# Scan units of 16 states by 63 positions in place of 8 states by 127

## The chip, the cores and the metric

The kernel runs on one core of one Trainium2 chip. The core has five engines with queues of their own: TensorE (PE in the profile, its weight loads PEld), VectorE (DVE), ScalarE (ACT), GpSimdE (POOL) and SyncE (SP, which here only issues DMAs). The metric is device time in microseconds, lower is better. Before the change the median of 3 runs is 32431.41 us (32428.44 to 32433.08).

## The reference

Input x is (8, 56, 56, 192), float32. The first layer (a gated Toeplitz convolution along rows and along columns, between two normalisations) is not touched by the change. The second is a selective scan in eight directions over the 3136 positions of each image. Cut to what matters, with DI = 384 channels, N = 16 states, K = 8 directions:

```python
def _selective_scan(u, delta, A, Bs, Cs, D):
    h0 = jnp.zeros(u.shape[:3] + (A.shape[-1],), u.dtype)
    def step(h, inp):
        ul, dl, bl, cl = inp
        dA = jnp.exp(dl[..., None] * A)
        h = dA * h + (dl * ul)[..., None] * bl[:, :, None, :]
        y = jnp.einsum('bkdn,bkn->bkd', h, cl)
        return (h, y)
    _, ys = jax.lax.scan(step, h0, (uL, dL, BL, CL))
```

u are the 384 channels after a 3x3 convolution, in the order of one direction; delta (softplus of a projection), B and C (16 values per position each) come from projections of u. Every channel has 16 states, each a first order recurrence along the positions. y, the states weighted with C and summed over the 16, goes on to a sum over directions, a layer norm, a gate and a projection.

## The kernel before, in words

**Stages.** The first layer takes the first tenth of the span. Then for each of the 8 images there is a scan stage (lines 484 to 922) and a layer norm stage (926 on), which writes the result and prepares the next image. The change is in the scan stage alone.

**Tiling of the scan.** Channels lie on partitions in NB = 3 blocks of 128. Positions are cut into chunks of W = 127, 25 in a direction; 4 chunks make a `Group` (7 groups in a direction, the last of one chunk). A `Unit` (710) is one chunk of one channel block with half of the states: 8 states by (1 + 127) positions, 1024 columns, the extra column holding the state before the chunk. A `Pair` (673) is two chunks of one channel block, so 4 units. One direction has 150 units, an image 1200, the kernel 9600. Units run pair after pair: both halves of chunk 0, both halves of chunk 1, then the next channel block.

**One unit, engine by engine.** PE makes the products delta\*u\*B (`products`, 716): the moved operand `bd` holds B on diagonals, the stationary operand `dut` holds delta\*u turned with positions on partitions, so a matmul over 64 positions spreads them to (states, positions). Positions 0 to 63 use partitions 0 to 63 (row group 0), the rest partitions 64 to 126 (row group 1). The result `bx` is 1024 float32 columns, two banks of PSUM; bank 0 holds states 0 to 3, bank 1 states 4 to 7, so each row group has something to write into both banks. The unit is therefore made in two turns of two matmuls: in turn 0 row group 0 writes bank 0 and row group 1 bank 1, in turn 1 the other way about. An ACT instruction stands between the turns (`turns_part`, 743, and `between`): it waits for turn 0, and turn 1 waits for it. ACT makes the decays `da` = exp(delta\*A) (line 687, one instruction a state and pair) and copies the state before the chunk into column 0 of every state of `bx` (`before`, 755); at the end of a pair it also keeps the last state in `carry` (`keep`, 773). DVE runs the scan (760) from `da` and `bx` into `h`. POOL multiplies `h` by C, spread over all partitions in `cbt`, into `hc` (`times_c`, 778). PE sums over states by 8 accumulating transposes (`sums`, 788) into `yps`, which ACT copies out (698) and SP stores to DRAM (708), 127 rows of 384 values each.

**What sets the order.** The order is written out by hand: a loop over steps t (871) emits, for every engine, parts of different units: turn 1 of unit t+1, turn 0 of unit t+2, the sums of unit t-3, `before` of unit t+1, the scan of unit t, `times_c` of unit t-1. Each engine runs its own instructions in that order and waits on semaphores. Exponentials are placed by a credit: 2.4 a step, 0.4 for each, less for other ACT work. `bx` has 3 buffers, `h` and `hc` 4, `da` 4, `dut` and `bd` 5, `cbt` 3, `yps` two halves of one bank, and one PSUM bank (`pmisc`) serves all other products.

**The front of a group** is planned by `Group.plan` (642) at steps before the group's first unit: load of `xs` (532), three projections `px` (539, copied out at 552), `to_dram` and `broadcast` of C (557, 563), B written to DRAM on diagonals (`diagonal_out`, 630, elements of 4 bytes) and read back (`diagonal_in`, 636), three matmuls `pd` for delta (574, copied out at 583), softplus (587), delta\*u on POOL (611), its transposes on PE (616) and the copy into `dut` (620). `do("SP", t)` puts the DMAs of a step behind its stores in SP's one queue.

Of the kernel before, what the change touches and what calls it, by code (L numbers as in the profile page):

```python
# [62 lines left out]
N = 16  # L63
# [3 lines left out]
NI = 10  # L67
W = 127
NG = -(-L // (4 * W))

# [14 lines left out]
def conv_kernel(ctx: ExitStack, tc: tile.TileContext, a: dict, out: bass.AP):  # L85
# [311 lines left out]
    for b in range(B):  # L397
# [86 lines left out]
        with ExitStack() as st:  # L484
            one = st.enter_context(tc.tile_pool(name="scan1", bufs=1))
            pre = st.enter_context(tc.tile_pool(name="front", bufs=2))
            blk = st.enter_context(tc.tile_pool(name="blk", bufs=5))
            hp = st.enter_context(tc.tile_pool(name="hp", bufs=4))
            cbp = st.enter_context(tc.tile_pool(name="cbp", bufs=3))
# [5 lines left out]
            das = [one.tile([128, 2, HN, W + 1], F32, name=f"da{i}") for i in range(4)]  # L495
            for t in das:
                nc.gpsimd.memset(t[:, :, :, 0], 0.0)
            yps = pyp.tile([W, 2, 2, 128], F32, name="yps")
# [3 lines left out]
            class Group:  # L502


                def __init__(self, k, g, i):
                    self.k, self.g, self.i = k, g, i
                    self.place, self.o, self.rev = DIRS[k]
                    self.nch = 4 if g < L // (4 * W) else 1
                    self.n = self.nch * W
                    u0 = g * 4 * W  # L510
                    self.m = min(self.n, L - u0)
                    self.p0 = L - u0 - self.m if self.rev else u0
                    self.ns = (self.nch + 1) // 2
                    self.ncs = self.nch // self.ns
                    self.w2 = self.ncs * W
                    self.cb, self.dut, self.bd = [], [], []
                    self.tag = "" if self.nch > 1 else "_last"
# [36 lines left out]
                def to_dram(self):  # L554
                    self.cd = cdp.tile([2, N, 2 * W], F32, name="cd")
                    for s in range(self.ns):
                        nc.sync.dma_start(
                            self.cd[s, :, : self.w2], self.pxs[48 : 48 + N, s * self.w2 : (s + 1) * self.w2]
                        )

                def broadcast(self, s):
                    cbt = cbp.tile([128, N, 2 * W], F32, name="cbt")
                    nc.sync.dma_start(
                        cbt[:, :, : self.w2],
                        self.cd[s : s + 1, :, : self.w2].to_broadcast([128, N, self.w2]),
                    )
# [3 lines left out]

# [19 lines left out]

# [16 lines left out]
                def product(self, c):  # L607
                    part = slice(c * W, (c + 1) * W)
                    xs = self.xs[:, :, ::-1] if self.rev else self.xs
                    self.du = pre.tile([128, NB, W], F32, name="du")  # L610
                    nc.gpsimd.tensor_mul(self.du, self.delta[:, :, part], xs[:, :, part])  # L611

                def turn(self, c):
                    self.pt = pmisc.tile([W, 512], F32, name="pt", tag="misc")
                    for d in range(NB):
                        nc.tensor.transpose(self.pt[:, d * 128 : (d + 1) * 128], self.du[:, d], ident)  # L616

                def turned(self, c):
                    dut = blk.tile([W, DI], F32, name="dut")
                    nc.scalar.copy(dut, self.pt[:, :DI])  # L620
                    self.dut.append(dut)

                def diagonal_out(self, c):
                    image = bdd[(self.i + c) % NI]
                    for h in range(2):
                        nr = min(64, W - 64 * h)
                        to = image[h]
                        to = bass.AP(to.tensor, to.offset, [[64, N], [64 * N + 1, nr], [1, 1]])
                        u = c * W + 64 * h
                        nc.sync.dma_start(  # L630
                            to, self.pxs[32 : 32 + N, u : u + nr].rearrange("n (s o) -> n s o", o=1)
                        )

                def diagonal_in(self, c):
                    bd = blk.tile([128, N, 64], F32, name="bd")
                    nc.sync.dma_start(
                        bd.rearrange("p n j -> p (n j)"),
                        bdd[(self.i + c) % NI].rearrange("h (s x) -> (h s) x", s=64),
                    )
                    self.bd.append(bd)  # L640

                def plan(self, at):

                    f = self.first

                    if self.nch == 1:
                        for d in range(NB):
                            at("PE", f - 23, self.project, d)
                        at("ACT", f - 22, self.projected)
                        at("SP", f - 22, self.to_dram)  # L650
                        at("PE", f - 21, self.all_steps)
                        at("late", f - 20, self.all_stepped)
                        start, out = f - 18, f - 22
                    else:
                        for d in range(NB):
                            at("PE", f - 22 + d, self.project, d)
                            at("PE", f - 18 + 2 * d, self.steps, d)
                            at("ACT", f - 17 + 2 * d, self.stepped, d)
                        at("ACT", f - 19, self.projected)
                        at("SP", f - 19, self.to_dram)  # L660
# [662 lines left out]
```

## Time and profile before

| what | value |
|---|---|
| median of 3 runs | 32431.41 us |
| span of the profiled execution | 32431.7 us |
| mean granted TensorE clock, core 0 | 0.974 |
| scan stage of one image, first to last scan (8 of them) | about 3125 us |
| busy share of the span: PE, DVE, ACT, POOL | 92%, 74%, 72%, 69% |
| DMA busy share in the scan stage, data rate | 0.43, 125 GB/s |
| DMA packets, all / under 512 bytes | 4696313 / 3677488 |

```profile
## 2 busy tenths in 40 slices
PE   8999899989999899989999899989998899989998
DVE  3444588858887588848887688848886688858886
ACT  2333588848887588848887588848886688848886
POOL 0000488838887588838887588838886688838885
```

The page cuts the span into 40 slices of some 811 us; a digit is the busy share of an engine in tenths. The first four slices are the first layer. After that the pattern repeats for eight images: 3 to 4 slices of scan, in which all engines but SP are at 0.8 or more, and a dip where the layer norm stage lies. Groups of instructions in the page have: line, engine, operation, output and inputs with partitions and elements, count, busy time and mean duration in ns of one, and the idle time of the engine just before them with what ended most of it. A timeline row has start and length in us, engine, line, what is done and how many instructions are merged in it; in brackets the idle time before it.

### The profile page before, as it was taken

To read this page: it belongs to the slowest core of one execution; us is meant where nothing else is said; L and a number is where in the kernel's file an instruction comes from. 1 tells how busy PE (TensorE), PEld (TensorE's weight loads), DVE (VectorE), ACT (ScalarE), POOL (GpSimd) and SP (SyncE) were. 2 spreads that over 40 slices of the span, in tenths; PEclk is the share of its full clock that TensorE was granted. 3 is DMA by queue.
4 is the path that set the end of the run, shared out by engine and by line. 5 is a ranking of instruction groups with operands and counts; after the bars stand their busy time and mean duration, and the time that the engine had idled before them with its cause. 6 is when DMAs were issued, how large, how long until landed. Compare 5 with 4: busy or idle time off the path is not lost. (4 is left out here: it accounts for less than half of the span.)

```text
span 32431.7 us, 535874 instructions
## 1 busy us (share of the span) xinstructions
PE 29974.2 (92%) x195376; PEld 20574.4 (63%) x195376; DVE 23854.0 (74%) x13460; ACT 23290.3 (72%) x63667; POOL 22357.6 (69%) x11632
## 2 busy tenths in 40 slices
PE   8999899989999899989999899989998899989998
PEld 5555566656666566656666566656666566656666
DVE  3444588858887588848887688848886688858886
ACT  2333588848887588848887588848886688848886
POOL 0000488838887588838887588838886688838885
PEclk9999999989999999989999999989999999999999
DMA  3222344444444444444444444444444444444444
GB/s 79 60 60 57 104 124 127 128 134 127 128 123 129 131 128 125 129 132 125 127 128 128 130 128 125 127 133 128 125 129 126 131 127 128 126 133 129 124 127 140
DMA packets 4696313, 3931.67 MB, mean 121 GB/s; under 512 B 3677488, under 2 KB 4379376, under 8 KB 4587824
## 3 DMA queue, kind: packets, MB, share of 16 engines
q1 hardware_dynamic: 4660528, 3890.16, 41.8%
q8 instruction: 1552, 25.43, 0.3%
q10 hardware_dynamic: 33152, 7.23, 0.2%
q14 instruction: 1081, 8.86, 0.1%
HBM read 3402.49 MB, written 508.64 MB: 121 GB/s over the span
## 5 line engine op out<-in xcount | busy, mean ns | idle before, releaser
L760 DVE TENSOR_TENSOR_SCAN h<-da,bx 128x1024 f32<-128x1024 f32 x9600 | 21446.0, 2275 | 3899.2 <-ACT bx L755 2988.2
L778 POOL TENSOR_TENSOR hc<-h,cbt 128x1016 f32<-128x1016 f32 x9600 | 20685.7, 2175 | 2449.0 <-DVE h L760 1924.3
L687 ACT ACTIVATE da<-delta,A_logs 128x254 f32<-128x254 f32 x39936 | 17114.9, 490 | 832.0 <-PE bx L732 785.1
L732 PE MATMUL bx<-bd,dut 63*128 63x252 f32 (+1 forms) x76800 | 11022.8, 404 | 1053.0 <-ACT bx L755 377.1
L788 PEld LDWEIGHTS yps<-ident,hc 128*127 128x127 f32 x76800 | 9249.2, 190 | 3383.4 <-issue 2106.3
L788 PE MATMUL yps<-ident,hc 128*127 128x128 f32 x76800 | 11068.5, 287 | 196.9 <-ACT bx L755 143.1
L732 PEld LDWEIGHTS bx<-bd,dut 64*128 64x128 f32 (+1 forms) x76800 | 6510.0, 187 | 4511.0 <-ACT da L687 876.4
L422 POOL MEMSET xp<- 128x58 f32 x12 | 1.3, 192 | 3406.1 <-DMA bd<-none 3406.1
L611 POOL TENSOR_TENSOR du<-delta,xs 128x381 f32<-128x381 f32 x1600 | 1602.1, 1002 | 745.2 <-ACT bx L755 478.8
L1022 POOL COPY xo<-xp 128x672 f32<-128x672 f32 x98 | 70.5, 749 | 2841.8 <-ACT xp L1005 2841.8
L539 PE MATMUL px<-xs,xpw 128*64 128x508 f32 (+1 forms) x2688 | 1304.9, 576 | 171.5 <-DMA xs<-xo 171.5
L574 PE MATMUL pd<-pxs,dtw 13*128 13x508 f32 x2304 | 1295.2, 641 | 18.2 <-ACT delta L583 10.7
L583 ACT COPY delta<-pd 128x508 f32<-128x508 f32 x1152 | 669.3, 581 | 726.4 <-PE pd L574 720.5
L755 ACT COPY bx<-h 128x8 f32<-128x8 f32 x4608 | 753.9, 164 | 592.7 <-PE bx L732 320.6
L773 ACT COPY carry<-h 128x8 f32<-128x8 f32 x4608 | 884.2, 192 | 343.4 <-DVE h L760 328.0
L755 ACT COPY bx<-carry 128x8 f32<-128x8 f32 x4992 | 820.7, 164 | 412.9 <-PE bx L732 381.9
L1005 ACT ACTIVATE xp<-pc,conv_b 128x448 f32<-128x448 f32 x147 | 93.5, 636 | 1352.1 <-PE pc L998 1352.0
L998 PE MATMUL pc<-xp,dg 128*128 128x448 f32 x2646 | 1019.5, 538 | 0.0
L698 ACT COPY yt<-yps 127x256 f32<-127x256 f32 (+1 forms) x2496 | 888.3, 356 | 154.3 <-PE yps L788 98.6
L1142 DVE SCALAR_TENSOR_TENSOR y<-xc,dsum,ysum 128x224 f32<-128x224 f32 x336 | 125.4, 443 | 1132.3 <-PE ysum L1123 1132.3
L620 ACT COPY dut<-pt 127x384 f32<-127x384 f32 x1600 | 757.9, 474 | 167.5 <-PE pt L616 123.6
L616 PE MATMUL pt<-ident,du 128*127 128x128 f32 x4800 | 815.7, 279 | 52.1 <-POOL du L611 36.2
(136 smaller groups left out, 16257.3 us busy)
## 6 DMA issues: line engine op xcount, KB each, us to landing
cbt<-cd SPq DMA_DIRECT2D x768, 2032.0 KB
bd<-bd SPq DMA_DIRECT2D x1600, 512.0 KB
yk<-yt SPq DMA_DIRECT2D x3584, 84.0 KB
xs<-xo SPq DMA_DIRECT2D x384, 762.0 KB
yt<-yt SPq DMA_DIRECT2D x1536, 190.5 KB
xo<-xo SPq DMA_DIRECT2D x168, 672.0 KB
cbt<-cd SPq DMA_DIRECT2D x64, 1016.0 KB
lt<-td SPq DMA_DIRECT2D x32, 1568.0 KB
```

The lines of the kernel that those rows point to most:

```text
L539: nc.tensor.matmul(self.px[:, : self.n], weights[self.k][0][:, d], self.xs[:, d], start=(d == 0), stop=(d == NB - 1),)
L574: nc.tensor.matmul(self.pd[:, : self.n], weights[self.k][1][:, d * 128 : (d + 1) * 128], self.pxs[0 : R + 1], start=True, stop=True,)
L611: nc.gpsimd.tensor_mul(self.du, self.delta[:, :, part], xs[:, :, part])
L687: yield nc.scalar.activation(da[:, : G.ncs, n, 1:], src.rearrange("p (c t) -> p c t", t=W), AF.Exp, scale=an[:, G.k, self.d, col : col + 1],)
L698: nc.scalar.copy(G.yt[:, : G.ncs, self.d * 128 : (self.d + 1) * 128], yps[:, self.i % 2, : G.ncs])
L732: mm = nc.tensor.matmul(self.bx[:, 4 * q : 4 * q + 4, 1 + 64 * r : 1 + 64 * r + nr], dut[rows, P.d * 128 : (P.d + 1) * 128], bd[rows, n0 : ...
L755: return nc.scalar.copy(self.bx[:, :, 0], prev)
L760: nc.vector.tensor_tensor_scan(self.h.rearrange("p n t -> p (n t)"), das[2 * (P.i % 2) + self.half][:, self.c].rearrange("p n t -> p (n t) ...
L773: nc.scalar.copy(P.carry[:, P.d, states(self.half)], self.h[:, :, W])
L778: nc.gpsimd.tensor_tensor(self.hc, self.h[:, :, 1:], G.cb[P.s][:, states(self.half), self.c * W : (self.c + 1) * W], ALU.mult,)
L788: nc.tensor.matmul(yps[:, self.P.i % 2, self.c], lhsT=self.hc[:, n], rhs=ident, start=(self.half == 0 and self.c == 0 and n == 0), stop=(s ...
L998: nc.tensor.matmul(pc, dg[:, d, j, :], xp[:, d, t * RT + dy : t * RT + dy + RT, dx : dx + HW], start=(j == 0), stop=(j == 8),)
```

## The change

W becomes 63, a chunk 63 positions (50 in a direction), a group 8 chunks. A unit now holds all 16 states of one chunk and channel block: again 16 x (1 + 63) = 1024 columns, and again 150 units in a direction. Two chunks form a pair for the front: `dut` has the first chunk in partitions 0 to 62 and the second in 64 to 126, and a copy with these halves exchanged (`swapped`) is made by two DMAs. `bd` is filled so that partitions 0 to 63 hold states 0 to 7 and partitions 64 to 127 states 8 to 15, for both chunks. So row group 0 makes states 0 to 7 of a unit, all in bank 0, and row group 1 states 8 to 15, all in bank 1: two matmuls of 504 columns, no turns, no ACT instruction between them.

The three channel blocks are interleaved, each one chunk behind the one before, so that a unit's predecessor in its own chain is three units back. `before` copies 16 columns from its `h` directly; `carry` and `keep` are gone. A block of exponentials covers 4 chunks of one channel block (252 elements an instruction, as before 254), and `da` is four times 4 chunks by 16 states. `hc` of two successive units lies side by side, so that one transpose of 126 columns sums both; 16 of them for two units, 8 a step. `yps` is copied out once for 4 units, and each unit's 63 rows of 128 values are stored by a DMA of their own.

Counts in one full group of 24 units, before and after: product matmuls 96 of 256 or 252 columns and 48 of 504; transposes for the sums 192 and 192; copies `before` 24 and 24 (8 and 16 columns); `keep` 12 and 0; exponentials 96 and 96; copies of `yps` 6 and 6; DMAs on SP: `diagonal_out` 8 and 8, `diagonal_in` 4 and 8, `swapped` 0 and 8, `broadcast` 2 and 4 (half the size), stores 4 and 24, `to_dram` 2 and 1, load 1 and 1.

```diff
-W = 127
-NG = -(-L // (4 * W))
+W = 63
+NC = -(-L // W)
+GC = 8
+NG = -(-NC // GC)
+SC = 4
...
-            blk = st.enter_context(tc.tile_pool(name="blk", bufs=5))
+            blk = st.enter_context(tc.tile_pool(name="blk", bufs=3))
             hp = st.enter_context(tc.tile_pool(name="hp", bufs=4))
+            hcp = st.enter_context(tc.tile_pool(name="hcp", bufs=3))
...
-            das = [one.tile([128, 2, HN, W + 1], F32, name=f"da{i}") for i in range(4)]
+            das = [one.tile([128, SC, N, W + 1], F32, name=f"da{i}") for i in range(4)]
...
-            yps = pyp.tile([W, 2, 2, 128], F32, name="yps")
+            yps = pyp.tile([2 * W, 2, 2, 128], F32, name="yps")
...
+                def swapped(self, p):
+                    dut = self.dut[p][0]
+                    other = blk.tile([128, DI], F32, name="dus")
                     for h in range(2):
+                        nc.sync.dma_start(other[64 * h : 64 * h + 64], dut[64 - 64 * h : 128 - 64 * h])
+                    self.dut[p].append(other)
...
+                        x = f - 24
+                        for d, s in enumerate((f - 18, f - 16, f - 12)):
+                            at("PE", s, self.steps, d)
+                            at("ACT", s + 1, self.stepped, d)
+                        at("late", f - 10, self.softplus)
+                    at("SP", x - 12, self.load)
+                    for d in range(NB):
+                        at("PE", x + d, self.project, d)
+                    at("ACT", x + 3, self.projected)
+                    at("SP", x + 3, self.to_dram)
+                    for p in range(self.npr):
+                        at("SP", x + 3 + p, self.diagonal_out, p)
+                        s = f - 8 + 6 * p
+                        at("POOL", s - 1, self.product, p)
+                        at("PE", s, self.turn, p)
+                        at("ACT", s + 1, self.turned, p)
+                        at("SP", s + 1, self.swapped, p)
+                        at("SP", s + 1, self.diagonal_in, p)
+                        at("SP", f + 6 * p - 5, self.broadcast, p)
...
+                def products(self):
+                    G, p, q = self.G, self.c // 2, self.c % 2
+                    self.bx = pb.tile([128, 2, HN, W + 1], F32, name="bx")
                     for r in range(2):
-                        q = (r + turn) % 2
-                        n0 = self.half * HN + 4 * q
-                        nr = min(64, W - 64 * r)
-                        rows = slice(64 * r, 64 * r + nr)
-                        mm = nc.tensor.matmul(
-                            self.bx[:, 4 * q : 4 * q + 4, 1 + 64 * r : 1 + 64 * r + nr],
-                            dut[rows, P.d * 128 : (P.d + 1) * 128],
-                            bd[rows, n0 : n0 + 4, :nr],
+                        rows = slice(64 * r, 64 * r + W)
+                        nc.tensor.matmul(
+                            self.bx[:, r, :, 1:],
+                            G.dut[p][q ^ r][rows, self.d * 128 : (self.d + 1) * 128],
+                            G.bd[p][rows, q, :, :W],
                             start=True,
                             stop=True,
                         )
-                        if turn:
-                            tc.add_manual_dep(mm.ins, self.between, IN_TURN, reason="bank")
...
+            for t in range(-2, len(units) + 10):
                 credit = min(credit, 0.0) + 2.4
                 if (U := unit(t + 2)) is not None:
-                    U.products(0)
+                    U.products()
+                for U, y in stores:
+                    U.store(y)
+                stores = []
+                for i in range(t, t + 3):
+                    U = unit(i)
+                    if U is not None and not U.ready and (U.prev is None or U.prev.h is not None):
+                        U.before(U.prev)
+                        credit -= 0.2
+                s = t - 4
+                if unit(s) is not None:
+                    if s % 2 == 0:
+                        sums(s, 0)
+                    else:
+                        sums(s - 1, 1)
+                        hcs.pop(s // 2)
+                s = t - 8
+                if unit(s) is not None and s % 4 == 0:
+                    y = pre.tile([2 * W, 2, 128], F32, name="yt")
+                    nc.scalar.copy(y, yps[:, s // 4 % 2])
                     credit -= 0.35
+                    stores = [(units[s + i], y[i % 2 * W : i % 2 * W + W, i // 2]) for i in range(4)]
                 credit -= 0.5 * do("ACT", t)
...
                 while must_exp(t):
                     one_exp()
+                while credit > 0.8 and may_exp(t):
+                    one_exp()
                 do("DVE", t)
                 if (U := unit(t)) is not None:
                     U.scan()
                 do("PE", t)
                 if (U := unit(t - 1)) is not None:
+                    if (t - 1) % 2 == 0:
+                        hcs[(t - 1) // 2] = hcp.tile([128, N, 2, W], F32, name="hc")
+                    U.times_c(hcs[(t - 1) // 2][:, :, (t - 1) % 2])
                 do("POOL", t)
                 do("SP", t)
```

## The prediction

> **What bounds the kernel now.** I read the stretches of the scan stage first, then the groups of instructions, then the timeline of single engines.
>
> ```profile
> 7286.00:10411.00 3125.00, 2977.11 (x20428) 2111.42 (x20427) 2680.48 (x1200) 2707.47 (x7629) 2766.19 (x1411) 1.00 0.43 125
> ```
>
> The columns are stretch, length, busy us of PE, PEld, DVE, ACT, POOL, clock, DMA share, GB/s. One image's scan takes 3125 us, 2.604 a unit. PE is busy 95% of it, the others 86 to 89%: PE is nearest to its limit, and four engines lie close together. Eight images: 25000 us.
>
> ```profile
> L760 DVE TENSOR_TENSOR_SCAN h<-da,bx 128x1024 f32<-128x1024 f32 x9600 | 21446.0, 2275 | 3899.2 <-ACT bx L755 2988.2 <-ACT da L687 383.9 <-PE bx L732 272.4
> L773 ACT COPY carry<-h 128x8 f32<-128x8 f32 x4608 | 884.2, 192 | 343.4 <-DVE h L760 328.0
> L755 ACT COPY bx<-h 128x8 f32<-128x8 f32 x4608 | 753.9, 164 | 592.7 <-PE bx L732 320.6 <-DVE h L760 255.0
> ```
>
> The scan stands idle 3899 us, three quarters of it for the 0.16 us copy into column 0, and that copy waits for products and an earlier scan. So a cheap link of a chain through three engines ends last.
>
> ```profile
> 10015.49 1.13 PE L732 MATMUL bx<-bd,dut 64*128 64x256 f32 x8
> 10016.55 1.15 PE L788 MATMUL yps<-ident,hc 128*127 128x128 f32 x8
> 10017.63 1.13 PE L732 MATMUL bx<-bd,dut 64*128 64x256 f32 x8
> 10018.69 1.15 PE L788 MATMUL yps<-ident,hc 128*127 128x128 f32 x8
> 10019.68 0.50 PE L616 MATMUL pt<-ident,du 128*127 128x128 f32 x3
> 10020.10 1.13 PE L732 MATMUL bx<-bd,dut 64*128 64x256 f32 x8
> ...
> 10030.18 0.70 PE L732 MATMUL bx<-bd,dut 64*128 64x256 f32 x4
> 10032.06 0.70 PE L732 MATMUL bx<-bd,dut 64*128 64x256 f32 x4 [1.19 <-DVE h L760]
> 10033.20 1.12 PE L788 MATMUL yps<-ident,hc 128*127 128x128 f32 x8 [0.44 <-ACT bx L755]
> ...
> 10040.18 1.07 PE L539 MATMUL px<-xs,xpw 128*64 128x508 f32 x2
> 10041.17 1.13 PE L732 MATMUL bx<-bd,dut 64*128 64x256 f32 x8
> ...
> 10049.78 1.11 PE L574 MATMUL pd<-pxs,dtw 13*128 13x508 f32 x2
> 10050.82 1.13 PE L732 MATMUL bx<-bd,dut 64*128 64x256 f32 x8
> ```
>
> By starts: products 1.06 us, sums 1.08, a plain unit 2.14; a turn adds 0.33 (2.47 from 10017.63 to 10020.10), px 0.99, pd 1.04. At 10030 the two turns (x4 each, where elsewhere x8 run through) fall apart, and PE waits.
>
> **PE's own sum.** A direction is 150 x 2.14 = 321.0 us; six full groups of 3 x 0.99 + 3 x 1.04 + 4 x 0.33 = 7.41 make 44.5; the short group has 0.80 + 0.86 + 0.33 = 2.0 (starts in its own rows near 9954 and 9959). 367.5 us, times 64: 23520. PE waits 25000 - 23520 = 1480 us. That is the most this change can take from waits; below it PE's work itself stands.
>
> ```profile
> 10032.99 6.64 DVE L760 TENSOR_TENSOR_SCAN h<-da,bx 128x1024 f32<-128x1024 f32 x3 [0.99 <-ACT da L687]
> 9942.74 21.32 POOL L778 TENSOR_TENSOR hc<-h,cbt 128x1016 f32<-128x1016 f32 x10
> 10042.36 3.29 ACT L687 ACTIVATE da<-delta,A_logs 128x254 f32<-128x254 f32 x8 [0.21 <-PE bx L732]
> ```
>
> Undisturbed, scans follow at (6.64 - 2.29) / 2 = 2.18 us, elsewhere up to 2.25: some 21100 us. POOL: (21.32 - 2.17) / 9 = 2.13, with 1600 products of 1.00 some 22050. Exponentials: (3.29 - 0.49) / 7 = 0.40; with copies, table loads and softplus ACT has some 327 us a direction, 20900. All below PE.
>
> **The change, part by part.**
>
> *Products.* Row groups overlap: single records at 10006.27, .59, .81 and 1.02 later carry one pass of each row group, 0.213 us for 256 columns, so 1.06 is 0.11 for the first weights, four passes and 0.10 to drain. Now two passes of 504 columns, 0.42 each: 1.05. Gain 0.015 x 9600 = 140 us.
>
> The kernel issues both passes of row group 0 before those of row group 1, and the records of the two first passes start 6 ns apart. The Trainium skill (TensorE: Matmul & The Clock Gate, Part 3) says that matmuls start and end strictly in program order. By that rule row group 1 starts only with the other's second pass, and a unit takes three passes, 1.46 us; the row disagrees, and my sum does without the rule.
>
> *The turns and the ACT instruction between.* This wait goes. Three `bx` buffers let PE begin unit t+3 when scan t ends; DVE then has two units, 4.4 us, and products with copy need some 1.4. So 3.0 us of lateness are covered, where before turn 0, an ACT instruction, turn 1 and the copy had to fit into one scan. Since PE's sum is above DVE's, DVE eats its stock and waits for PE; PE waits for nobody. I take back all 1480, less what follows.
>
> *Chains.* The predecessor ends three units earlier, so the copy of column 0 waits for its products alone. It is queued ahead of the exponentials on ACT: they stand behind it while PE makes the products. 16 columns for 8: between nothing and another 0.16 us; an exponential of 254 elements takes 0.49, so I take 0.01, hidden in ACT's slack. `keep` gone: 4608 x 0.10 us, off the path: 0 (460 gained if ACT were the bound). ACT after: 320 us a direction of PE's 365.
>
> *`yps`.* Its halves share a bank. The copy is queued behind the sums of the next pair, the second half of these sums behind the copy. ACT stands some 0.9 us per copy, 37 a direction, 33 us: 353 of 365, still covered, but hardly.
>
> *Softplus.* With its table loads 1.28 + 1.47 + 1.28 = 4.03 us on ACT, against 0.35 spare a step: ACT is 3.7 late. Where a `yps` copy stands behind it, the sums can absorb about 1.9, and PE waits 1.8; this falls so in half of the directions. 384 x 0.9 = 350 us; bounds 0 and 384 x 4.03 = 1550.
>
> *Short groups.* 48 exponentials of 0.32, softplus 3.05 and copies 1.8 are 20.3 us of ACT in six units, where PE has 14.8: 5.5 x 64 = 350; bounds 0 and twice that.
>
> *POOL.* Runs of 63 in place of 127, 16 for 8. No row shows the price of a run. A copy of 672 elements in 12 runs takes 749 ns, so a run costs between 0 and 62 ns; I take 6, 0.05 a unit: 2.35 with the products, under PE's 2.43.
>
> *DMAs.*
>
> ```profile
> L708 SPq DMA_DIRECT2D yt<-yt x1600: 216/531/6541, 3706.9 to 32157.5; - x178
> L630 SPq DMA_DIRECT2D bd<-pxs x3200: 303/677/7692, 3637.6 to 32092.0; - x189
> 10020.37 17.80 SPq L708 DMA_DIRECT2D yt<-yt x3
> ```
>
> SP issues 54 a group in place of 21. By medians (0.53 a store, 0.68 `diagonal_out`, 0.55 the reads and, as nearest row, the swaps, 0.76 `broadcast`, 3.6 the load) that is 34 us of 58. `swapped` waits for ACT's copy, with reads and broadcast queued behind it; landing is due five steps, 12 us, later. Cost 0; without cover see the second rival.
>
> *Ends of an image.* Sixteen exponentials before the first scan in place of eight, 3.2 us, a swap, and chains that run out: some 8 us x 8 = 60.
>
> **Sum.** 32431.7 - 25000 + 23520 - 140 + 350 + 350 + 60 = 31570 us. The span, 32431.7, is the median of 32431.41 but for 0.3. The sum's own range, with softplus and short groups between their bounds for the most part, is 31100 to 32150.
>
> **Rivals.**
>
> *ACT takes PE's place.* For: 353 of 365 us, and copies that block the exponentials behind them. Against: ACT late no longer idles. If each step loses 0.25 us more, a direction is 391, as now (25000 / 64): 32450.
>
> *SP late, the slower side.* The three stores at 10020 held SP 5.9 us each; the mean of a queue that backs up decides. From 58 / 54 = 1.08 us SP is the bound, from 62.5 / 54 = 1.16 the kernel is slower; at 1.3, twice the medians, a full group is 70 us, 6.25 x 64 of them 28000, the time 35400. Against: 127 rows of a store trickled over 16 us at a DMA share of 0.07, one engine's worth; 63 rows can be split evenly.
>
> *Row groups in series.* 1.46 in place of 1.05: 9600 x 0.41 = 3900, 35500. Against: the row groups overlap now, and nothing but the length differs.
>
> *POOL's runs.* From 17 ns a run POOL is the bound, from 38 the kernel is slower, at 62 it has 2.80 a unit: 26900, time 34300.
>
> *No waits at all.* 30870, if ACT's lags are absorbed.
>
> **How the numbers follow.** Forecast 0.60; no waits 0.08; ACT 0.10; SP 0.08; POOL 0.05; series 0.04; a wait I haven't seen, slower, 0.05. Two in a thousand, 65 us, is what this measurement can tell from no change. Faster: 0.58 + 0.08 + 0.04 (ACT) + 0.02 (POOL) = 0.72; same 0.05; slower 0.23. The range 30850 to 32700 leaves out most of the slower rivals, some 0.17, and little below.
>
> **What would show it.** Right: products of some 1.05 us in four records, PE above 97% busy in the scan stage, the scan's idle time released by products or copies at PE's pace, stages of about 3000 us. Wrong: scans or sums that wait for DMAs or POOL, SP issues with a mean over 1.1 us, `times_c` above 2.3 us, products above 1.2, or PE rows with gaps released by the copy of `yps`.

## The result and the profile after

The changed kernel takes 34835.51 us (median of 4 runs, 34818.07 to 34856.32), the kernel before beside it 32431.65 us: a ratio of 1.0742, with a 95% interval of 1.0727 to 1.0758. The forecast was 31570 us. The change costs 2404 us where it was to save 860.

First the stretches, as before. The columns are stretch, length, busy us of PE, PEld, DVE, ACT and POOL with their instructions, granted clock, DMA share, GB/s. The first row is the scan stage of the second image; the others are groups 0 to 3 of one direction (24 units each), from the start of one scan to that of another.

```profile
7595.02:11022.04 3427.02, 3007.93 (x15604) 1598.81 (x15604) 2653.87 (x1199) 2611.32 (x7031) 2737.52 (x1403) 0.94 0.48 125
...
12802.44:12899.38 96.94, 67.80 (x312) 34.96 (x310) 53.03 (x26) 55.12 (x149) 57.44 (x30) 0.85 0.35 95
12899.38:12978.82 79.44, 66.33 (x322) 35.19 (x320) 52.92 (x26) 53.84 (x143) 55.22 (x29) 0.89 0.43 109
12978.82:13038.29 59.47, 57.49 (x313) 30.63 (x312) 53.04 (x26) 53.29 (x142) 53.13 (x29) 1.00 0.56 142
13038.29:13097.97 59.68, 57.62 (x314) 30.54 (x312) 53.33 (x25) 51.20 (x138) 54.74 (x29) 1.00 0.55 146
```

And the same stretches of the kernel before, groups 0 and 2:

```profile
12069.42:12139.56 70.14, 62.23 (x417) 42.34 (x417) 53.90 (x25) 56.38 (x164) 56.76 (x30) 1.00 0.38 117
...
12201.06:12262.18 61.12, 59.19 (x411) 42.15 (x410) 53.58 (x25) 53.55 (x151) 55.28 (x30) 1.00 0.45 131
```

Group 2 became shorter, 59.47 for 61.12 us. Group 0 takes 96.94 and group 1 79.44 us, with all but the same work: ACT is busy 55.12 us in group 0 and 53.29 in group 2, DVE 53.03 and 53.04. So in group 0 no engine is short of time: PE is busy 70% of it, and ACT 57%. Where the time went is a matter of order.

The Trainium skill (Perfetto Trace Analysis, "Identifying the Most-Contended Engine") says to find the engine with the highest occupancy and to work on that one first. For PE it does not count the busy time of matmuls; it takes the busy share of the weight loads, and the arithmetic done as a share of the peak, which was not worked out here. Weight loads are busy 36% of group 0 (34.96 us), so the rule gives POOL with 59%. POOL is not what the others wait for first: in the wait rows below it waits 3956.8 us for DVE itself.

Averaged over all images, from the starts of the scans, us a unit in groups 0 to 6 of directions 2 to 8:

| kernel | 0 | 1 | 2 | 3 | 4 | 5 | 6 (six units) |
|---|---|---|---|---|---|---|---|
| before | 2.83 | 2.53 | 2.55 | 2.55 | 2.55 | 2.58 | 2.79 |
| after | 4.06 | 3.14 | 2.41 | 2.47 | 2.48 | 2.44 | 3.09 |

Groups 2 to 5 gain 24 x (0.14 + 0.08 + 0.07 + 0.14) = 10 us a direction; groups 0, 1 and 6 lose 24 x (1.23 + 0.61) + 6 x 0.30 = 46. The first direction of an image loses 0.36 a unit on average, 54 us, in its groups 0 and 1 (4.26 for 2.64 and 3.57 for 2.55) and a little in group 6. Together some (7 x 36 + 54) x 8 = 2450 us, the whole difference.

Now the timeline of ACT and of DVE at the start of a direction. A row has start and length in us, engine, line, what is done and how many; in brackets the idle time before it and what ended it.

```profile
8895.81 0.19 ACT L734 COPY bx<-h 128x16 f32<-128x16 f32 x1 [3.55 <-PE bx L723]
8895.93 0.67 ACT L560 ACTIVATE pxs<-px,px_bias 64x504 f32<-64x504 f32 x1
8896.51 6.42 ACT L702 ACTIVATE da<-delta,A_logs 128x252 f32<-128x252 f32 x16
8902.83 0.17 ACT L734 COPY bx<-h 128x16 f32<-128x16 f32 x1
8907.46 0.19 ACT L734 COPY bx<-h 128x16 f32<-128x16 f32 x1 [4.46 <-PE bx L723]
...
8913.85 0.19 ACT L734 COPY bx<-h 128x16 f32<-128x16 f32 x1 [2.06 <-PE bx L723]
8913.98 0.57 ACT L587 COPY delta<-pd 128x504 f32<-128x504 f32 x1
8914.45 5.64 ACT L702 ACTIVATE da<-delta,A_logs 128x252 f32<-128x252 f32 x14
8919.99 0.17 ACT L734 COPY bx<-h 128x16 f32<-128x16 f32 x1
```

```profile
8903.02 8.82 DVE L738 TENSOR_TENSOR_SCAN h<-da,bx 128x1024 f32<-128x1024 f32 x4 [6.28 <-issue]
8920.18 2.29 DVE L738 TENSOR_TENSOR_SCAN h<-da,bx 128x1024 f32<-128x1024 f32 x1 [8.34 <-ACT bx L734]
```

ACT makes 16 exponentials in one run, then the copy that a scan waits for; four scans follow at full pace. Meanwhile ACT makes only two exponentials and a few copies, and waits 4.46, 1.70 and 2.06 us for PE. The next run of 14 comes just before the next block's first scan, and DVE stands 8.34 us. Four scans and a stall, again and again. The wait rows (us in all, times, the longest):

```profile
DVE h L738 <- ACT bx L734: 4705.1, 1784, 10.3
POOL hc L749 <- DVE h L738: 3956.8, 912, 22.7
PEld bx L723 <- DVE h L738: 3942.6, 2315, 7.4
...
ACT bx L734 <- PE bx L723: 3334.3, 2636, 11.4
...
PE bx L723 <- DVE h L738: 2746.4, 872, 7.1
```

DVE waits for ACT, ACT for PE, PE for DVE: a ring, in which nobody works ahead.

In a steady stretch PE is what the forecast saw:

```profile
10008.79 0.69 PE L723 MATMUL bx<-bd,dus 63*128 63x504 f32 x1
10008.80 0.69 PE L723 MATMUL bx<-bd,dut 63*128 63x504 f32 x1
10009.32 0.58 PE L723 MATMUL bx<-bd,dus 63*128 63x504 f32 x1
10009.33 0.58 PE L723 MATMUL bx<-bd,dut 63*128 63x504 f32 x1
10009.84 1.09 PE L835 MATMUL yps<-ident,hc 128*126 128x128 f32 x8
10010.86 0.69 PE L723 MATMUL bx<-bd,dut 63*128 63x504 f32 x1
...
10012.93 0.69 PE L723 MATMUL bx<-bd,dus 63*128 63x504 f32 x1
```

Products 1.05 us (10008.79 to 10009.84), sums 1.02, a plain unit 2.07 (10010.86 to 10012.93).

**The mechanism to be tested.** A block's 16 exponentials fill one of the four `da` buffers. Three channel blocks are under way at once, each with a buffer, so one buffer is left to run ahead with: the exponentials of block i may be emitted only after the last unit of block i-4, and must be out one step before its first unit (lines 811 to 818). By the order of the units that leaves 6 steps for every block of a full group. At a direction's end the short group's blocks are two chunks long and hold a whole buffer each, blocks begin 2 steps apart in place of 4, and the steps left are 4 for the first block of the next direction, 2 for the short group's last and 2 for the next direction's fourth. What isn't out by then is forced, all in one step, behind that step's column-0 copies. Each costs 0.4 of the credit of 2.4 a step, and what is overdrawn is carried on (`min(credit, 0.0) + 2.4`): so in the next steps nothing is made ahead, and the next block is forced too. Following the loop, 863 of an image's 4992 exponentials are forced: where the second direction begins 3, 11 (the short group's last block), 16, 14, 12, 10, 13, 9, 6 and 4 at the heads of successive blocks, and hardly any in groups 2 to 5 (at most 3 a direction, in group 2). The order of exponentials and column-0 copies on ACT in the traces is the one that the loop gives (followed through the first image of every run). I call the runs "bursts" and the overdrawn credit "debt".

### The profile page after: what moved, and what is told of

The parts are those of the page before. It is cut to its first block, busy times and chain, and to the rows that moved or that the text cites. A ratio compares the mean times of both kernels' runs of the same rounds, so it can differ in the third digit from the quotient of the medians.

```text
span 34830.9 us, 473357 instructions
## 1 busy us (share of the span) xinstructions
PE 30277.1 (87%) x156976; PEld 16476.7 (47%) x156976; DVE 23676.0 (68%) x13460; ACT 22543.9 (65%) x58955; POOL 22154.0 (64%) x11592
## 5 line engine op out<-in xcount | busy, mean ns | idle before, releaser
L749 POOL TENSOR_TENSOR hc<-h,cbt 128x1008 f32<-128x1008 f32 x9600 | 20512.7, 2169 | 4271.5 <-DVE h L738 3956.8
L702 ACT ACTIVATE da<-delta,A_logs 128x252 f32<-128x252 f32 (+1 forms) x39936 | 16435.2, 489 | 5.6
L723 PE MATMUL bx<-bd,dus 63*128 63x504 f32 x19200 | 11288.7, 670 | 2682.7 <-DVE h L738 2679.7
L835 PEld LDWEIGHTS yps<-ident,hc 128*126 128x126 f32 x76800 | 8599.6, 145 | 7854.7 <-issue 4818.3
L723 PE MATMUL bx<-bd,dut 63*128 63x504 f32 x19200 | 11296.7, 670 | 81.6 <-DVE h L738 66.7
L835 PE MATMUL yps<-ident,hc 128*126 128x128 f32 x76800 | 10942.6, 288 | 266.2 <-ACT yt L869 235.7
L723 PEld LDWEIGHTS bx<-bd,dus 63*128 63x128 f32 x19200 | 2995.8, 195 | 4689.6 <-DVE h L738 3606.0
L734 ACT COPY bx<-h 128x16 f32<-128x16 f32 x9408 | 1695.0, 181 | 4555.2 <-PE bx L723 3257.6
L723 PEld LDWEIGHTS bx<-bd,dut 63*128 63x128 f32 x19200 | 2995.9, 195 | 1271.5 <-issue 920.5
L614 POOL TENSOR_TENSOR du<-delta,xs 128x378 f32<-128x378 f32 x1600 | 1587.1, 992 | 1550.1 <-ACT bx L734 1377.5
L869 ACT COPY yt<-yps 126x256 f32<-126x256 f32 x2400 | 891.0, 371 | 1917.0 <-PE yps L835 1794.0
```

The lines of the kernel that those rows point to most:

```text
L614: nc.gpsimd.tensor_mul(self.du[:, :, :, :W], self.delta[:, :, part].rearrange("p d (c t) -> p d c t", t=W), xs[:, :, part].rearrange("p d ...
L702: yield nc.scalar.activation(da[:, : self.nc, n, 1:], src.rearrange("p (c t) -> p c t", t=W), AF.Exp, scale=an[:, G.k, self.d, n : n + 1],)
L723: nc.tensor.matmul(self.bx[:, r, :, 1:], G.dut[p][q ^ r][rows, self.d * 128 : (self.d + 1) * 128], G.bd[p][rows, q, :, :W], start=True, st ...
L734: nc.scalar.copy(self.bx.rearrange("p r n t -> p (r n) t")[:, :, 0], src)
L749: nc.gpsimd.tensor_tensor(hc, self.h[:, :, 1:], self.G.cb[self.c // 2][:, :, q * W : (q + 1) * W], ALU.mult)
L835: nc.tensor.matmul(yps[:, t // 4 % 2, t // 2 % 2], lhsT=hcs[t // 2][:, n].rearrange("p c t -> p (c t)"), rhs=ident, start=(n == 0), stop=( ...
```

## The experiments

Each run is compared with the kernel before on the same chip. In the expectations a "place" is the step from one scan's start to the next within a group, counted from 0 to 23.

### Debt, buffers, the place in ACT's queue, and the swaps

Edits, each made alone in the changed kernel:

```diff
e1_no_debt
-                credit = min(credit, 0.0) + 2.4
+                credit = 2.4
e2_five_da (yt and the short group's xs, pxs and delta have one buffer, to make room)
-            das = [... for i in range(4)]
+            das = [... for i in range(5)]
-                return P.i < 4 or t > blocks[P.i - 4].end
+                return t > P.G.first - 10 and (P.i < 5 or t > blocks[P.i - 5].end)
e3_exps_first
+                while must_exp(t):
+                    one_exp()
                 for U, y in stores:
                     U.store(y)
...
-                while must_exp(t):
-                    one_exp()
e4_no_swap
-                        at("SP", s + 1, self.swapped, p)
-                            G.dut[p][q ^ r][rows, self.d * 128 : (self.d + 1) * 128],
+                            G.dut[p][0][rows, self.d * 128 : (self.d + 1) * 128],
```

No debt, expected:

> Edit: the credit that places the exponentials starts at 2.4 in each step instead of carrying a debt over; nothing else. Theory 'bursts' (blocks of 16 exponentials, too few da buffers for three interleaved chains, and a credit debt that keeps later blocks from being made ahead, so that all 16 stand in ACT's queue just ahead of the scan that needs them): in the emitted order the exponentials that are forced in the step before their block fall from 863 to 311 an image, and about three bursts of 11 a direction stay of eight. The loss in the first two groups of a direction, some 46 us a direction now, falls to about 18: 34830 - 64 x 28 = 33000 us. Theory 'DMAs' (swapped halves, reads and stores late): no change, 34800. Theory 'ACT's queue' (exponentials stand behind the copy of column 0, which waits for products): little change, above 34300.

Measured 32477.54 us, ratio 1.0015 (1.0005 to 1.0024). One line takes back 2358 of the 2404 us, more than was expected. Two stretches, groups 0 and 1 of the same direction as above:

```profile
12075.59:12156.33 80.74, 65.71 (x319) 34.33 (x317) 53.03 (x26) 58.10 (x157) 57.54 (x30) 0.89 0.41 115
12156.33:12215.80 59.47, 56.70 (x307) 29.97 (x307) 53.33 (x26) 52.82 (x141) 53.61 (x29) 1.00 0.53 132
```

Group 1 is as short as any; group 0 still has 80.74 us (75.6 on average over directions 2 to 8). Bursts remain there (311 forced exponentials an image), but they no longer breed the next one.

Five buffers, expected:

> Edit: five da buffers in place of four (with single buffers for the short group's xs, pxs and delta and for yt, to make room; exponentials not before their group's softplus); the credit as in the changed kernel. Theory 'bursts': with a block more to run ahead the forced exponentials in the emitted order fall from 863 to about 166 an image and no step has more than 5 of them, so the stalls of 6 to 10 us at the head of each block go. The first two groups come to some 2.5 to 2.6 us a unit as the others: 34830 - 64 x 45 = 31950 us, between 31600 and 32300. Theory 'DMAs': no change, 34800. Theory 'ACT's queue': no change above 1%, since the copies stand where they stood.

Measured 32512.60 us, 1.0024 (1.0014 to 1.0034): right in kind, 560 us short of the expected and outside its range. The debt is still carried; but with the steps left at 4 or more everywhere, little is forced at the start of directions 2 to 8 (groups 0 and 1: 2.91 and 2.49 us). In the loop as it ran 229 exponentials an image are forced, not 166, and 126 of them in the first direction, up to 16 in a step. The first direction of each image, where no run-ahead is possible, still has 2.98 a unit where the others have 2.50 to 2.60; with no debt it has 2.57. So in directions 2 to 8 the loss needs both, a window too short and a debt that carries it on, and either cure takes most of it; in the first direction, which starts with nothing made ahead, the debt alone carries it.

Forced exponentials first, expected:

> Edit: the forced exponentials are emitted ahead of the copies of column 0 of the same step instead of behind them. Theory 'bursts': the burst of up to 16 x 0.40 = 6.4 us stays, but starts before the products of that step are made: some 1.3 us less for each of about 8 bursts a direction, 64 x 8 x 1.3 = 650 us: 34200. Theory 'ACT's queue': the wait in front of the exponentials is the cause, so most of the loss goes: below 33000. Theory 'DMAs': no change.

Measured 33276.78 us, 1.0261 (1.0246 to 1.0276), better than "bursts" had it and worse than its rival. The same 863 exponentials are forced. Only their order against ACT's other work of the same step differs, and 1560 us are gone: two thirds of the 2404 us, and half of the some 3000 us that the slow groups cost. So half of the bursts' price is the queue: copies that wait for products stand ahead of exponentials that could run at once, which is the idle time of 3.55 us ahead of the run of 16 and of 2.06 us ahead of the run of 14 in the rows above.

No swaps (one of the two row groups of each unit then reads the other chunk's half of `dut`, so half of the states get the products of a neighbouring chunk), expected:

> Edit: the DMAs that exchange the halves of dut are left out and all products read dut itself, so the second half of the states gets the products of the other chunk; the work of all engines stays. It takes away 3200 DMAs and SP's wait for ACT that stands ahead of the reads of bd. Theory 'bursts' and theory 'ACT's queue': no change, 34600 to 34850. Theory 'DMAs': the loss at the start of each direction falls, below 33500.

Measured 34833.24 us, 1.0739 (1.0723 to 1.0755): nothing. The 3200 DMAs of `swapped` are free. This run leaves the other DMAs in place; that they are not the cause either is shown by the runs without debt and with the exponentials first, which change no DMA and take the loss, or two thirds of it, away.

### What sets the short group apart

```diff
e10_half_short_exps
-                    for n in range(N):
+                    for n in range(0, N, 1 + G.last):
...
-                    left = N
+                    left = HN if exps and exps[0][0].G.last else N
```

> The changed kernel with everything as it was, debt, four buffers and the place in the queue, but the short group of each direction makes the exponentials of 8 of its 16 states only: 24 for its six units, as many a unit as the full groups make, in place of 48. That leaves out 1.5 thousand of 39.9 thousand exponentials, at 0.395 us from one to the next 24 x 64 x 0.395 = 0.6 ms of ACT's time. 'The short group is the trigger' (its 48 in six steps run the credit into debt, and groups 0 and 1 of the next direction pay): groups 0 and 1 of directions 1 to 7 come down to what groups 2 to 5 take, 38.6 + 16.6 + 4.7 = 60 us a direction, 34835 - 60 x 56 = 31480; the first direction of each image keeps its own. 31400 to 32300. Rival 'only the work counts': 34830 - 600 = 34230. Rival 'a direction's start is slow of itself (new weights, the first column from another tile)': above 34000 with group 0 at 3.5 us a unit or more.

Measured 34272.10 us, where the kernel before had 32577.33 on that chip: 1.0522 (1.0506 to 1.0537), against 1.0742. That is 2.2%, some 710 us, hardly more than the work that is left out. My reading of the trigger fell. Groups 0 and 1 of the direction whose rows are above:

```profile
12643.55:12730.91 87.36, 66.69 (x318) 35.05 (x317) 53.03 (x25) 52.66 (x142) 57.68 (x30) 0.88 0.41 109
12730.91:12806.90 75.99, 65.66 (x318) 34.43 (x316) 52.92 (x25) 53.77 (x142) 55.24 (x29) 0.90 0.45 114
```

On average group 0 has 3.81 and group 1 3.09 us a unit. It isn't mainly the number of the short group's exponentials that starts the bursts. The other thing that is special there are the windows: they are set by when blocks begin and end, and this run leaves them as they were, 2 and 4 steps for whole blocks of 16. Following the loop again, 9, 7, 11, 9, 12, 8, 5 and 3 are still forced at the heads of the next direction's blocks. The run with five buffers, which widens the windows and leaves the numbers, agrees. The rival that a direction's start is slow of itself had its sign here, too (above 34000, group 0 over 3.5 us); against it stands the same run with five buffers, which has the same weights and first columns and 2.91 us in group 0. The expectation was written without looking at the windows; they would have told it.

### Does the kernel before pay for its debt too?

```diff
b1_before_no_debt (in the kernel before)
-                credit = min(credit, 0.0) + 2.4
+                credit = 2.4
```

> The kernel before with no debt carried (credit set to 2.4 at every step): does the kernel before lose to the same thing? It emits exponentials by halves of 8, and its group 0 takes 2.83 us a unit where groups 1 to 4 take 2.54, group 6 2.79: 0.29 x 24 + 0.25 x 6 = 8.5 us a direction, 0.54 ms in all. 'Debt costs before too': 32150 (31900 to 32300). Rival 'halves of 8 run far enough ahead, and its groups 0 and 6 are slow for their own reasons (the start, the short group)': 32430 within 40.

Measured 33562.80 us, 1.0349 (1.0334 to 1.0365): 1130 us slower, the opposite of what was expected. Group 0 does gain (2.83 to 2.73), but groups 1 to 5 go from 2.55 to about 2.7, most of it at one place of the group, 3.7 to 5.9 us. ACT there, first in the kernel before, then without debt:

```profile
12247.91 1.28 ACT L587 ACT_TABLE_LOAD   x1
12249.21 1.47 ACT L587 ACTIVATE delta<-delta 128x1524 f32<-128x1524 f32 x1
12250.59 0.16 ACT L755 COPY bx<-h 128x8 f32<-128x8 f32 x1
12250.77 1.28 ACT L687 ACT_TABLE_LOAD   x1
```

```profile
12592.38 1.28 ACT L587 ACT_TABLE_LOAD   x1
12593.68 1.47 ACT L587 ACTIVATE delta<-delta 128x1524 f32<-128x1524 f32 x1
12595.17 1.28 ACT L687 ACT_TABLE_LOAD   x1
12596.46 0.91 ACT L687 ACTIVATE da<-delta,A_logs 128x254 f32<-128x254 f32 x2
12597.27 0.15 ACT L755 COPY bx<-h 128x8 f32<-128x8 f32 x1
```

Softplus is charged 3.0 credits, and its debt keeps exponentials out of the next step. Without it two exponentials and the table load that they need come ahead of the copy, which is 2.2 us later. So debt is no fault as such: after softplus it does its work. Nor is a chain of forced exponentials dear of itself. Following the loop of the kernel before in the same way, 574 of an image's 4992 are forced, in runs of up to 8 all through group 0, and 173 without debt. Yet group 0 took only 2.83 us a unit there, and lost 0.10 of it without debt. There the exponentials come by halves of 8 for one channel block at a time; that this is what keeps the chain cheap was not tried.

### Softplus a step earlier

```diff
e6_no_debt_softplus (against no debt)
-                        at("late", f - 10, self.softplus)
+                        at("late", f - 11, self.softplus)
```

> Four buffers, no debt, softplus one step earlier: against the run with no debt only softplus moves. 'Softplus late' (POOL's product of delta and x waits for it, the turn on PE waits for POOL, and the next products wait behind the turn): 32478 - 0.96 ms = 31520 (31300 to 31900). Rival 'the stall moves along' (the column-0 copy behind softplus in ACT's queue is what ends late, and does so a step earlier as well): 32480 within 100.

Measured 32774.99 us, 1.0105 (1.0090 to 1.0120), 300 us slower than with no debt alone. The stall of 4.8 us moved from place 13 to place 12 (5.0), as the rival said; beyond that places 0 and 1 rose from 2.2 and 2.7 to 2.8 and 3.1 in the later groups, which neither theory had and which I haven't traced.

### Together

```diff
e7_no_debt_exps_first: e1 and e3
e5_five_da_no_debt_softplus: e1, e2 and softplus at f - 11
e8_no_debt_but_softplus: e7, and
-                credit = 2.4
...
-                credit -= 3.0 * do("late", t)
+                credit = 2.4 - 2.8 * do("late", t)
e9_five_da_exps_first: e8 and e2
```

> Four buffers, no debt, and the forced exponentials ahead of the column-0 copies of the step. In the run with no debt group 0 still takes 3.15 us a unit where groups 1 to 5 take 2.49: 0.66 x 24 x 64 = 1.0 ms. Alone, the place in ACT's queue had taken 1.56 of the 2.4 ms that the change lost against before, and no debt 2.36 of them. 'Place' (a burst costs because the copy waits for nothing while exponentials wait behind it): some 60 per cent of the 1.0 ms go, 31850 (31600 to 32100). Rival 'ACT has no time left in group 0, wherever they stand': 32480 within 100; ahead of the copies they may also delay the copy of the next scan and lose: above 32550.

Measured 32009.69 us, 0.9870 (0.9854 to 0.9887): in the expected range, faster than the kernel before.

> Five buffers of exponentials, no debt carried from step to step, and softplus one step earlier (emitted at the end of step f-11 in place of f-10). Theory 'bursts' (exponentials forced together ahead of a block's first scan, behind the column-0 copy): what is left in the run with five buffers is the first direction of each image (2.98 us a unit where the others have 2.55: 0.43 x 150 = 64 us an image, 0.5 ms) and group 0 of the other directions (2.91 where group 2 has 2.51: 0.40 x 24 x 56 = 0.54 ms); both come from debt and go. 'Softplus': in the run with no debt the scans at places 13 and 14 of groups 1 to 4 take 4.8 and 3.6 us where their neighbours take 2.4; of these 3.6 us some 2.5 go when softplus comes a step earlier: 2.5 x 6 groups x 64 = 0.96 ms. Both right: 32512 - 1.04 ms - 0.96 ms = about 30550, at most 31100. Bursts alone: 31500. Softplus alone: 31550. Rival 'the sums of ACT or PE are the floor now' (two different changes have already ended at 32480 and 32510): 32400 or more.

Measured 32148.45 us, 0.9914 (0.9899 to 0.9929), far from 30550. The first direction came down to 2.6 us a unit as foretold, but places 12 and 13 have 5.0 and 3.5 us: softplus a step earlier gives nothing here either.

> The run with four buffers, no debt and the forced exponentials first, but with the debt of softplus kept (the step after softplus makes no exponentials). 'Debt after softplus is worth its price': with all debt kept, places 13 to 16 of groups 2 to 4 took 4.8, 2.2, 2.2 and 2.7 us; without any, 4.8, 3.6, 2.2 and 2.2, so 0.9 us a group more: 32010 - 0.9 x 6 x 64 = 31660 (31450 to 31850). Rival 'exponentials pushed out of that step come back as forced ones in group 0': 32010 or more.

Measured 31947.56 us on the same chip as the run with half of the short group's exponentials: 0.9808 (0.9793 to 0.9823), 0.6% below the run without softplus's debt, where 1.1% was expected. Places 13 to 16 are 4.8, 2.2, 2.2 and 2.5 again; group 0 gave a little back, 3.00 for 2.93.

> The same with five buffers of exponentials. 'Run-ahead' (group 0 is still slow because the short group's 48 exponentials can't be made early enough with one buffer free): group 0 goes from 2.93 to 2.6 us a unit and the short group from 2.7 to 2.2, (0.33 x 24 + 0.5 x 6) x 64 = 0.7 ms under the run with four: about 31000 (30800 to 31500). Rival 'ACT has no time left at a direction's start, whatever the order': the same as with four buffers, within 100. Rival 'earlier exponentials stand in front of the copies of the next group's preparation' (places 0, 1 and 10 of groups 1 to 4 took 3.0 us with five buffers where they take 2.2 to 2.7 with four): half of the gain is given back, 31350.

Measured 31894.77 us on that chip, 0.9789 (0.9773 to 0.9806), the fastest of all, but far from the 31000 expected, and the intervals of the last two overlap. Group 0 went down to 2.61 as foretold and group 6 to 2.40, where 2.2 was expected, 11 us a direction; groups 1 to 5 gave some 8 us of them back (2.52, 2.58, 2.48, 2.51 and 2.56 for 2.43, 2.48, 2.48, 2.48 and 2.45), mostly at places 0 and 10 to 12, and the first direction rose from 2.53 to 2.61. By the places that is the last rival, and more than the half it had named. Groups 0 and 1, one direction:

```profile
11935.57:11999.61 64.04, 60.01 (x320) 31.89 (x319) 53.02 (x25) 53.71 (x148) 57.60 (x30) 0.97 0.57 149
11999.61:12058.11 58.50, 56.60 (x307) 29.89 (x307) 53.22 (x26) 52.87 (x141) 52.33 (x28) 1.00 0.55 138
```

Group 0 does the same work as in the changed kernel's rows, ACT 53.71 us of it, in 64.04 in place of 96.94 us. So with this order of exponentials the changed kernel is about 2.1% faster than the kernel before, and as it stands 7.4% slower. The kernel before was not given the exponentials-first order, so how much of the 2.1% the tiling alone is worth is not shown.

## Why the prediction was wrong

**Products: right.** 1.05 us forecast and measured, four records as described. The row groups' first passes start 0.01 us apart, at 10008.79 and 10008.80, although the kernel calls for row group 0's matmul, both of its passes, ahead of row group 1's; "row groups in series" is out.

**The steady groups: right in sum, with two misses that cancel.** The forecast had 24 x 2.125 + 7.4 + 0.9 = 59.3 us for a full group, the last two terms being the turns, px, pd and softplus. Groups 2 to 5 took 57.8, 59.3, 59.5 and 58.6. The sums were 0.06 us a unit cheaper than taken, 1.4 a group, and softplus dearer: in groups 2 to 4 place 13 stands 2.4 us above its neighbours, where 0.9 was the term. That these two cancel was luck.

**Chains: the step that failed.** It said of the copy of column 0: "It is queued ahead of the exponentials on ACT: they stand behind it while PE makes the products", and gave this wait no price. The 0.01 beside it, "hidden in ACT's slack", is for the copy's 16 columns in place of 8. The cover was judged by ACT's sum, 353 of 365 us. But slack in a sum helps only if ACT may use it at the right time, and whether it may is decided by the buffers of `da` and the credit, which no step of the prediction looked at, though both stood in the diff: a block of 16 for a half of 8, three channel blocks in flight for one, four buffers as before. In its place the runs showed up to 16 exponentials at once ahead of a block's first scan, and scans that start 6 to 10 us late: 46 us a direction and 54 in an image's first, some 3 ms. The runs without debt, with five buffers and with the exponentials first each take it away in a different manner.

**"PE waits for nobody": wrong for the same reason.** PE was busy 3007.93 of 3427.02 us, 88%. The stock of two units that was to cover 3.0 us of lateness met scans 6 to 10 us late: the places where group 0's blocks begin took 8.6 to 12.0 us, where 2.2 is undisturbed.

**Short groups: sized well, placed wrongly.** 14.8 + 5.5 = 20.3 us were forecast for its six units, and they took 18.6. What the short blocks do to the next direction's windows had no term. Halving their exponentials left the next direction's group 0 at 3.81 us a unit, so it isn't mainly their ACT time.

**The rest held.** `times_c` took 2169 ns for 1008 elements, 2175 for 1016 before, 2.15 and 2.14 ns an element: the shorter runs cost next to nothing, and POOL's rival is out. SP was no bound:

```profile
L758 SPq DMA_DIRECT2D yt<-yt x9600: 264/322/3633, 3712.3 to 34566.1; - x196
...
L639 SPq DMA_DIRECT2D dus<-dut x3200: 487/588/1839, 3652.6 to 34528.5; - x189
```

(least, median and longest in ns) a store is 0.32 and a swap 0.59 us; over the second image's scan stage all issues on SP took 0.52 us on the mean, where 1.1 was the sign of trouble. The `yps` copy blocked ACT for its products (1794.0 us in all before line 869), but groups 2 to 5 held their pace with it.

**The rivals.** "ACT takes PE's place" was the nearest: ACT does set the end, yet by order and not by being full. The rival even names "copies that block the exponentials behind them", but it was priced at a loss spread over every step, and 32450 as its worst. "A wait I haven't seen, slower" had 0.05. The signs listed as wrong were waits for DMAs and POOL, SP, dear products and the `yps` copy: none came in a size that explains the loss. POOL waited 239 us in all for DMAs, the sums' weight loads 992 us for POOL (816 before) and 671 for the `yps` copy. So that list would not have found the cause; PE's busy share, in the list of signs of being right, points to it.

## What to carry to other kernels

Where a schedule is written out by hand, a change of tiling is also a change of every placement rule in it: follow the rule through one start and one end of the loop, with the new sizes of burst and buffer, before trusting an engine's sum. ACT, at 97% by its sum, idled 43% of group 0: this can happen when an engine's work comes due in bursts, its queue is in order, and the instruction in front waits for another engine. Ask of each buffer ring how many steps it leaves to work ahead, at its narrowest place, and of each budget what happens after it has been overdrawn once.

## What the runs showed of the hardware

**The clock falls with the stalls.** In group 0 the granted clock is 0.85, in groups 2 and 3 1.00 (rows above); over the program 0.933 for 0.974 before. After an idle time of PE of 6.03 us the first passes of 504 columns are 1.21 us in place of 0.69:

```profile
8905.36 1.21 PE L723 MATMUL bx<-bd,dus 63*128 63x504 f32 x1 [6.03 <-DVE h L738]
...
8912.69 0.69 PE L723 MATMUL bx<-bd,dus 63*128 63x504 f32 x1
```

The Trainium skill (TensorE: Matmul & The Clock Gate, "HAM oscillation — how this bites in real kernels") says that idle gaps of more than some 3.4 us on PE bring the clock to half. The trace agrees for long gaps: the first passes behind this one take 1.75 times as long, and of PE's 408 idle times of 3 us or more in the scan stages 395 have a fall of the clock in them or within 1 us behind. So have 64 of the 184 between 2 and 3 us, which the rule doesn't foretell. The slower clock lengthens the ring just when it is late. In the scan stages it stood at half for 3287 us, 116 before; at most half of that, 1.6 ms of the loss, is the clock's own (an estimate), and no run separates it.

**Weight loads of 127 columns.** For the transposes of the scan stage, 128 columns took 142 ns, 126 took 145, and 127, in the kernel before, 190 to 194:

```profile
L835 PEld LDWEIGHTS yps<-ident,hc 128*126 128x126 f32 x76800 | 8599.6, 145 | 7854.7 <-issue 4818.3 <-POOL hc L749 992.2 <-ACT yt L869 671.0
...
L623 PEld LDWEIGHTS pt<-ident,du 128*128 128x128 f32 x4800 | 559.5, 142 | 529.0 <-POOL du L614 517.2 <-issue 11.8
```

The number alone does not decide it: in the kernel before the products' loads of 128 columns took 187 ns and the first layer's transposes, with 128 columns, 200. The sums, eight such loads and transposes, went from 1.08 to 1.02 us with the change from 127 to 126; that the one comes of the other wasn't tried by itself.
